# A third buffer for the gated products, some rescales moved to ScalarE, and a convolution of 28 block products in two parts

## The chip, the cores and the metric

The kernel runs on one core of a Trainium2 chip. A core has a matrix engine (TensorE, PE in the profile; its weight loads are shown apart as PEld), a vector engine (VectorE, DVE), a scalar engine (ScalarE, ACT), a general engine (GpSimd, POOL) and a queue engine (SyncE, SP). PE reads its operands from on-chip memory (SBUF) and writes into accumulators (PSUM) of 8 banks, each 128 partitions by 512 float32. The metric is the time of one execution in microseconds on the device; before the change it is 2197.08 us, the median of 3 runs (2196.97 to 2197.81).

## The reference

The input is two sequences of 1024 rows with 1024 features, so 2048 rows. One "macaron" layer is computed in float32:

```python
x = x + 0.5 * ffn(layernorm(x))
x = x + s4(layernorm(x))
x = x + 0.5 * ffn(layernorm(x))
```

`ffn` is `(silu(x @ Wg) * (x @ Wu)) @ Wd`, with Wg and Wu of 1024 x 2752 and Wd of 2752 x 1024. The weights come as 4-bit numbers, eight in a word, with a scale and a zero point for each group of 128 input rows and each column: `W = (w4 - (z4 + 1)) * s`.

`s4` is a causal convolution along the feature axis, `irfft(rfft(u, 2L) * rfft(K, 2L), 2L)[:L] + D * u` with L = 1024. The response K comes from 64 complex poles; it is the same for all rows. A causal convolution of length 1024 is a product with a lower triangular Toeplitz matrix, and in blocks of 128 x 128 that matrix has eight different blocks, one for each distance from the diagonal.

## The kernel before

Rows are worked in blocks b of 512. The list `JOBS` (L1232) holds eight jobs, (b, 1) for the first feed-forward of a block and (b, 3) for its second; j counts them from 0. Each job has a gate/up stage (`gate_up`, L602) and a down stage (`down`, L678).

The gate/up stage has 40 steps (`STEPS`, L38): 8 waves of columns, each over 8 groups g of input rows. A wave has three tiles f of 128 hidden columns (waves 0 to 4) or two (waves 5 to 7), and each tile has two units, gate (even number) and up (odd). The last wave has one more unit, the 64 columns that are left of gate and up together. In each step each unit gets two matmuls of 512 columns, one with the low part of the input (xTl, float16) and one with the high part (xTh, float32r), into the unit's own PSUM bank. The weights in SBUF are the small integers, so after each group the bank is multiplied by the ratio of this group's scale to the next one's: this is the rescale, `scaled` (L596), on ACT (L598) or DVE (L600). Even units go to ACT and odd ones to DVE; in job 0 the unit at position 1 goes to ACT when g is a multiple of 4 (L639).

After the last group of a wave `gated` (L651) makes the product with the sigmoid for each tile: ACT makes g = silu(gate) (L653), DVE multiplies it with the up unit into hf (L656), POOL casts hf into hh (L658) and subtracts to get the low part hl (L660). hf has two buffers (`hfpool`, L101), so the third hf of a wave is written once POOL is done with the first. `gated_half` (L663) does the same for the unit of 64 + 64 columns, with hf_half from the same pool (L670) and the two parts on DVE (L672, L673).

The down stage has 2 x 22 steps (a, f). Each adds hl and hh of tile f, times the weights of f, to four banks c = 0 to 3 (L689), and each bank is rescaled after it: even c on ACT, odd c on DVE (L697).

PE works in the order in which its instructions are written into its queue, and so do ACT, DVE, POOL and SP. That order is set when the program is built: a scheduler goes by the order of the code and by when it expects operands to be ready, so that an instruction may stand some way ahead of its place in the code. Some stretches are fixed by hand with `in_order_of_writing`. Work beside the matmuls is hung on step numbers, `at(up, s, f)` and `at(dn, d, f)`; it is written before the step's matmuls. Each step also issues the load of one weight tile on SP four steps ahead (L558, L565) and its cast three steps ahead, on POOL (L576) apart from a part of job 0.

The work that hangs on steps and that the change touches:

- `first_weights` (L516): job 0 unpacks all weights; its last part falls into job 0's down stage.
- `s4_tables` (L951): in job 1, one piece a step from step 2 on, the response K and the tables of the convolution. `s4_response` (L899) makes K by a transform with a cosine and a sine table (32 passes of PE, L907), scales it, adds D and writes it to DRAM. `s4_toeplitz` (L924) reads it back so that each partition is shifted by one, turns it with two matmuls (L942) into `toeplitz`, and makes the differences `after` and `ahead` (L949).
- In jobs 1, 2, 5 and 6 the s4 of the block before: for each tile t of 128 rows, the normalization at step 8 + 4t, the transposes `turn_whole` at step 10 + 4t and `convolve` (L961) at step 12 + 4t; in job 1 all of it 30 steps later. So `convolve` runs 16 times.

`convolve` makes the first four output blocks with four products (L968; 512, 384, 256 and 128 columns wide) and the last four with thirteen (L987): products of the diagonal kind, products with differences of blocks, and three products with sums of neighbouring input blocks, which POOL makes (L980). All are float32, which PE runs as two passes each. Counted in blocks of 128 columns they are 31 block products. DVE adds the results to x with three instructions (L976, L1003, L1006). PSUM banks that no unit holds are handed out in turn (`bank`, L111).

Of the kernel before, what the change touches and what calls it, by code (L numbers as in the profile page):

```python
# [23 lines left out]
P = 128  # L24
# [30 lines left out]
def macaron_s4_kernel(  # L55
# [45 lines left out]
    hfpool = ctx.enter_context(tc.tile_pool(name="hf", bufs=2))  # L101
# [500 lines left out]
    def gate_up(j, b, hooks):  # L602
        hi, lo = pieces[b]
        ps = {}
        for s, (wi, g) in enumerate(STEPS):
# [13 lines left out]
            for k, pos, done in turns:  # L619
# [18 lines left out]
                if g < GK - 1:  # L638
                    on_act = unit % 2 == 0 or (j == 0 and pos == 1 and g % 4 == 0)  # L639
# [38 lines left out]
    def down(j, b, hooks):  # L678

        steps = [(a, f) for a in range(NH) for f in range(NF)]  # L680
        for d, (a, f) in enumerate(steps):
# [5 lines left out]
            for c in range(4):  # L687
# [9 lines left out]
                on_act = c % 2 == 0  # L697
# [20 lines left out]
    toeplitz = const.tile([P, HID], F32, tag="toeplitz", name="toeplitz")  # L718

    blocks = toeplitz.rearrange("p (d m) -> p d m", d=NC)  # L720
    after = const.tile([P, 3, P], F32, tag="after", name="after")
    ahead = const.tile([P, 3, P], F32, tag="ahead", name="ahead")
# [176 lines left out]
    def s4_response():  # L899
# [4 lines left out]
        ps = bank("s4_k")  # L904
        for r in range(8):
            for i in range(2):
                nc.tensor.matmul(  # L907
                    ps[:, r : r + 1],
                    tables[i].rearrange("p (a r) -> p r a", r=8)[:, r, :],
                    s4["se"][:, i, r : r + 1],  # L910
                    start=(i == 0),
                    stop=(i == 1),
                )
        k = t4("s4_response")
        d, none = k[:1, 8:9], k[:1, P : 2 * P - 1]
        nc.sync.dma_start(d, dskip.unsqueeze(0))
        nc.gpsimd.memset(none, 0.0)
        nc.vector.tensor_scalar(k[:, :8], ps[:, :8], 1.0 / HID, None, ALU.mult)
        nc.vector.tensor_tensor(k[:1, 0:1], k[:1, 0:1], d, ALU.add)
        nc.sync.dma_start(k_dram[:, : P - 1], none)  # L920
        nc.sync.dma_start(k_dram[0, P - 1 :].rearrange("(a r) -> a r", r=8), k[:, :8])
        s4.clear()

    def s4_toeplitz():  # L924

        both = [t4("s4_rows"), t4("s4_turn")]
        rows, turn = both[0], both[1][:, :P]
# [12 lines left out]
        for i in range(NH):  # L940
            ps = bank(f"s4_t{i}")
            nc.tensor.matmul(ps, turn, rows[:, bass.ts(i, 512)], start=True, stop=True)  # L942
            dst = toeplitz[:, bass.ts(i, 512)]
            if i:
                nc.vector.tensor_copy(dst, ps)
            else:
                nc.scalar.copy(dst, ps)
        for dst, d in ((after, 3), (ahead, 1)):
            nc.vector.tensor_tensor(dst, blocks[:, d : d + 5 : 2], blocks[:, 2:7:2], ALU.subtract)  # L949
# [11 lines left out]
    def convolve(b, t, s, name):  # L961
# [4 lines left out]
        ps = bank(f"pc_{name}_0")  # L966
        for c in range(4):
            nc.tensor.matmul(  # L968
                ps[:, P * c :],
                s[:, c, :],  # L970
                toeplitz[:, : 512 - P * c],
                start=(c == 0),
                stop=(c == 3),
            )
        part = x[b][t][:, :512]
        nc.vector.tensor_tensor(part, part, ps, ALU.add)  # L976

        sums = ypool.tile([P, TB], F32, tag="y", name=f"sums_{name}")
        sums = sums[:, : 3 * P].rearrange("p (c t) -> p c t", c=3)
        nc.gpsimd.tensor_tensor(sums, s[:, 0:6:2, :], s[:, 1:6:2, :], ALU.add)  # L980
        own = bank(f"pc_{name}_1")
        both = bank(f"pc_{name}_2")[:, : 2 * P].rearrange("p (y m) -> p y m", y=2)
        flat = own.rearrange("p (y m) -> p y m", y=4)
        upper, lower = flat[:, 0:4:2], flat[:, 1:4:2]
# [4 lines left out]
        for y in range(2):  # L989
            product(flat[:, 2 * y : 2 * y + 2], s[:, 4 + 2 * y, :], blocks[:, 0:2], start=(y == 0))  # L990
        for y in range(2):
            product(flat[:, 2 * y + 1], s[:, 5 + 2 * y, :], blocks[:, 0])
        for i in range(3):
            y = slice(max(0, i - 1), 2)
            d = slice(max(0, 1 - i), 3 - i)
# [238 lines left out]
    def fast():  # L1234
        for j, (b, k) in enumerate(JOBS):
# [7 lines left out]
            if prev:  # L1243
# [3 lines left out]
                if pk == 1:  # L1247
# [11 lines left out]
                    def conv(t):  # L1259
                        convolve(pb, t, s4x.pop(t), f"{pb}_{t}")  # L1260
# [211 lines left out]
```

## Time and profile before

| what | value |
|---|---|
| median of 3 runs | 2197.08 us |
| the profiled execution, its span | 2195.57 us, 2193.7 us |
| rescales in gate/up on ACT, on DVE | 1224 of 660 ns, 1184 of 694 ns |
| rescales in down on ACT, on DVE | 640 of 662 ns, 640 of 698 ns |
| hf (DVE), hh and hl (POOL) | 168 of 749 ns, 623 ns and 1297 ns |
| passes of the convolution, 512 / 384 / 256 / 128 columns | 32 / 32 / 288 / 192 |
| granted PE clock over the run | 0.993 |

Busy times of PE can overlap, since the end of a matmul is modelled and the next one starts before it; the distance from start to start tells what one costs. A line of the timeline gives the start, the length, the engine, the source line, the operation, the tiles written and read, how many instructions are merged, and in brackets how long the engine stood before it and what released it. A line of the waits gives who waited for whom, the microseconds in total, how many times, and the longest.

### The profile page before, as it was taken

What the parts mean: (1) busy time and instruction counts of PE and PEld (TensorE: products, weight loads), DVE (VectorE), ACT (ScalarE), POOL (GpSimd) and SP (SyncE); (2) the same over time, 40 slices, a digit from 0 to 9 for tenths busy, and PEclk for the clock granted to TensorE, in tenths of its full rate; (3) what the DMA queues carried; (4) which work ended last, traced back from release to release, by engine and by line L of the source; (5) the groups of instructions that cost most, each with busy time, mean ns of one, the idle gap of its engine ahead of it and who ended that gap; (6) DMA issues with size and microseconds to landing.
All of it is one profiled execution on the core that took longest, in us unless ns stands there. A gap on an engine that the chain in (4) does not pass through costs nothing.

```text
span 2193.7 us, 29717 instructions
## 1 busy us (share of the span) xinstructions
PE 2119.6 (97%) x9524; PEld 1421.1 (65%) x9524; DVE 1720.4 (78%) x2826; ACT 1404.9 (64%) x2197; POOL 1015.0 (46%) x1334
## 2 busy tenths in 40 slices
PE   5999899999999999999999999999999999999998
PEld 3555665566867568655775558676686766865576
DVE  7889889778887877778777787867778677777776
ACT  5877466446754677666767667646776466767765
POOL 3868734444334453455334553435534345345642
PEclk9999999999999999999999999999999999999999
DMA  4433321112111211211321121112111121121111
GB/s 139 120 96 111 105 69 32 54 49 74 38 40 46 93 45 46 79 34 33 107 71 46 31 71 35 41 51 72 37 34 42 49 93 36 54 81 36 33 33 57
DMA packets 163681, 132.43 MB, mean 60 GB/s; under 512 B 22395, under 2 KB 151172, under 8 KB 163518
## 3 DMA queue, kind: packets, MB, share of 16 engines
q1 hardware_dynamic: 162670, 129.12, 19.4%
q8 instruction: 77, 1.26, 0.2%
q10 hardware_dynamic: 592, 1.25, 0.1%
q14 instruction: 86, 0.70, 0.1%
q0 software_dynamic: 256, 0.10, 0.0%
HBM read 104.79 MB, written 25.50 MB: 59 GB/s over the span
## 4 chain that ended last, share of the span: by engine, by line
PE 84%; DVE 7%; POOL 4%; issue 2%; DMA 1%; SPq 1%; ACT 0%; POOLq 0%; DVEq 0%; ACTq 0%
PE pg L628 50%; PE po L689 26%; PE pc L987 3%; DVE pg L600 2%; PE pc L968 1%; PE pb L711 1%; POOL hl L660 1%; PE pt L219 1%; DVE po L600 1%; DVE hf L656 1%; POOL w_up L576 1%; PE st L219 1%; POOL w_down L576 1%; POOL hh L658 1%; DVE rawd L461 0%
## 5 line engine op out<-in xcount | busy, mean ns | idle before, releaser
L598 ACT ACTIVATE pg<-pg,rat 128x512 f32<-128x512 f32 x1224 | 778.6, 660 | 472.3 <-PE pg L628 471.3
L600 DVE TENSOR_TENSOR pg<-pg,rat 128x512 f32<-128x512 f32 x1184 | 788.0, 694 | 167.5 <-PE pg L628 163.2
L628 PE MATMUL pg<-xTh,w_up 128*128 128x512 f32 x2752 | 878.5, 444 | 11.9 <-DVE pg L600 9.4
L628 PE MATMUL pg<-xTl,w_up 128*128 128x512 f16 x2752 | 731.1, 384 | 14.7 <-DVE w_up L572 6.6
L576 POOL CAST w_up<-b 128x768 fp32r<-128x768 int8 (+2 forms) x487 | 376.0, 774 | 614.0 <-PE pg L628 470.6
L628 PEld LDWEIGHTS pg<-xTh,w_up 128*128 128x128 f32 x2752 | 519.7, 190 | 203.0 <-DVE pg L600 41.7
L689 PE MATMUL po<-hl,w_down 128*128 128x512 f32 x1344 | 540.6, 405 | 15.4 <-DVE po L600 9.7
L598 ACT ACTIVATE po<-po,ratd 128x512 f32<-128x512 f32 x640 | 421.4, 662 | 175.1 <-PE po L689 175.1
L689 PE MATMUL po<-hh,w_down 128*128 128x512 f32 x1344 | 523.6, 393 | 0.0
L600 DVE TENSOR_TENSOR po<-po,ratd 128x512 f32<-128x512 f32 x640 | 441.6, 698 | 93.6 <-PE po L689 89.1
L628 PEld LDWEIGHTS <-w_up 128*128 128x128 bf16 x2752 | 228.3, 99 | 344.1 <-issue 165.2
L576 POOL CAST w_down<-bd 128x512 fp32r<-128x512 int8 x352 | 220.6, 628 | 422.3 <-PE po L689 366.2
L689 PEld LDWEIGHTS po<-hl,w_down 128*128 128x128 f32 x1344 | 252.9, 189 | 94.1 <-DVE po L600 23.9
L689 PEld LDWEIGHTS po<-hh,w_down 128*128 128x128 f32 x1344 | 254.0, 189 | 46.0
L660 POOL TENSOR_TENSOR hl<-hf,hh 128x512 fp32r<-128x512 f32 x168 | 218.0, 1297 | 7.9
L656 DVE SCALAR_TENSOR_TENSOR hf<-pg,rat,g 128x512 f32<-128x512 f32 x168 | 124.2, 749 | 86.7 <-ACT g L653 44.6
L653 ACT ACTIVATE g<-pg,rat 128x512 f32<-128x512 f32 x168 | 111.0, 687 | 45.9 <-PE pg L628 36.3
L658 POOL CAST hh<-hf 128x512 fp32r<-128x512 f32 x168 | 104.7, 623 | 61.4 <-PE pg L628 41.1
L182 DVE BATCH_NORM_STATS2 stats<-x 128x6 f32<-128x512 f32 x96 | 63.6, 677 | 1.0
L219 PE MATMUL pt<-ident,xn 128*128 128x128 f32 x256 | 44.2, 293 | 10.3 <-ACT xn L1339 7.6
L242 DVE TENSOR_TENSOR xTl<-pt,xTh 128x512 f16<-128x512 f32 x56 | 38.3, 688 | 13.7 <-ACT xTh L241 12.9
L219 PEld LDWEIGHTS pt<-ident,xn 128*128 128x128 f32 x256 | 34.8, 151 | 21.1 <-ACT xn L1339 9.2
(163 smaller groups left out, 957.2 us busy)
## 6 DMA issues: line engine op xcount, KB each, us to landing
b<-wq SPq DMA_DIRECT2D x319, 96.0 KB
bd<-wdq SPq DMA_DIRECT2D x336, 64.0 KB
x<-in_L_attn_u_dram SPq DMA_DIRECT2D x30, 512.0 KB
b<-wq SPq DMA_DIRECT2D x128, 64.0 KB
xs<-x SPq DMA_DIRECT2D x16, 512.0 KB
x<-xs SPq DMA_DIRECT2D x16, 512.0 KB
out_dram<-x SPq DMA_DIRECT2D x16, 512.0 KB
b<-wq SPq DMA_DIRECT2D x64, 80.0 KB
```

What stands on the lines that cost most here:

```text
L182: nc.vector.bn_stats(stats[:, t, i, :], x[b][t][:, bass.ts(i, 512)])
L219: nc.tensor.transpose(ps[:, bass.ts(k, P)], n[:, bass.ts(k, P)], ident)
L576: nc.gpsimd.tensor_copy(t, b)
L598: nc.scalar.activation(dst, src, AF.Copy, scale=sc)
L600: nc.vector.tensor_tensor(dst, src, sc.to_broadcast([P, TB]), ALU.mult)
L628: nc.tensor.matmul(p, weights, (lo, hi)[k][:, g, :], start=(g == 0 and not done), stop=(g == GK - 1 and done), skip_group_check=True,)
L653: nc.scalar.activation(g, pg, AF.Silu, scale=rat[:, 2 * f, GK - 1 :])
L656: nc.vector.scalar_tensor_tensor(hf, pu, last, g, ALU.mult, ALU.mult)
L658: nc.gpsimd.tensor_copy(hi, hf)
L660: nc.gpsimd.tensor_tensor(lo, hf, hi.bitcast(F32), ALU.subtract)
L689: nc.tensor.matmul(ps[c], w[:, bass.ts(c, P)], part, start=(f == 0 and k == 0), stop=(f == NF - 1), skip_group_check=True,)
L987: nc.tensor.matmul(dst, lhsT, rhs, start=start, stop=stop, skip_group_check=True)
```

## The change

Five edits:

- `hfpool` gets three buffers instead of two.
- In gate/up, job 1 sends the rescale of position 1 to ACT in steps 0 to 31 when g is even (16 rescales). Job 0 stays as it was.
- In the down stage of job 0, the rescale of c = 1 goes to ACT when f is even (20 rescales; the step f = 20 has none).
- The convolution is built from 28 block products in 24 matmuls: 4 of 256 columns, 20 of 128. It is a generator in two parts. The first (output blocks 0 to 3, 7 products) runs at the old step, the second (output blocks 4 to 7, 17 products) one step later. POOL makes three instructions of sums instead of one, and DVE adds the results with two instructions in the first part and three in the second. The tables are `near`, `after`, `ahead` and `middle` instead of the whole `toeplitz`, made once from the same rows.
- The response is made as one row on one partition, with its operands swapped on PE, in two banks of 512 with one evacuation each, and goes to DRAM as one row.

In the general path, which runs only when the inputs are out of range, one small tile moves to another pool and the convolution's parts run one after the other.

```diff
-    hfpool = ctx.enter_context(tc.tile_pool(name="hf", bufs=2))
+    hfpool = ctx.enter_context(tc.tile_pool(name="hf", bufs=3))
...
-                    on_act = unit % 2 == 0 or (j == 0 and pos == 1 and g % 4 == 0)
+                    on_act = unit % 2 == 0
+                    if pos == 1:
+                        on_act = (j == 0 and g % 4 == 0) or (j == 1 and s < 32 and g % 2 == 0)
...
-                on_act = c % 2 == 0
+                on_act = c % 2 == 0 or (j == 0 and c == 1 and f % 2 == 0)
...
-        ps = bank("s4_k")
-        for r in range(8):
-            for i in range(2):
-                nc.tensor.matmul(
-                    ps[:, r : r + 1],
-                    tables[i].rearrange("p (a r) -> p r a", r=8)[:, r, :],
-                    s4["se"][:, i, r : r + 1],
...
+        for half in range(2):
+            ps = bank(f"s4_k{half}")
+            for r in range(4):
+                for i in range(2):
+                    nc.tensor.matmul(
+                        ps[:1, bass.ts(r, P)],
+                        s4["se"][:, i, 4 * half + r : 4 * half + r + 1],
+                        tables[i].rearrange("p (a r) -> p r a", r=8)[:, 4 * half + r, :],
...
+            nc.vector.tensor_scalar(
+                k[:1].rearrange("p (a r) -> p r a", r=8)[:, 4 * half : 4 * half + 4],
...
-        nc.sync.dma_start(k_dram[0, P - 1 :].rearrange("(a r) -> a r", r=8), k[:, :8])
+        nc.sync.dma_start(k_dram[:, P - 1 :], k[:1])
...
+        blocks = whole.rearrange("p (d m) -> p d m", d=NC)
+        nc.vector.tensor_copy(near[:, 0:3], blocks[:, 0:3])
+        nc.vector.tensor_copy(near[:, 3], blocks[:, 4])
         for dst, d in ((after, 3), (ahead, 1)):
-            nc.vector.tensor_tensor(dst, blocks[:, d : d + 5 : 2], blocks[:, 2:7:2], ALU.subtract)
+            own = dst[:, 0:3]
+            nc.vector.tensor_tensor(own, blocks[:, d : d + 5 : 2], blocks[:, 2:7:2], ALU.subtract)
+            nc.vector.tensor_tensor(dst[:, 3], dst[:, 2], dst[:, 1], ALU.subtract)
+            nc.vector.tensor_tensor(dst[:, 2], dst[:, 0], dst[:, 1], ALU.subtract)
+        for i in range(2):
+            src = blocks[:, 2 + 4 * i]
+            nc.vector.tensor_tensor(middle[:, i], src, blocks[:, 4], ALU.subtract)
...
-        nc.gpsimd.tensor_tensor(sums, s[:, 0:6:2, :], s[:, 1:6:2, :], ALU.add)
+        nc.gpsimd.tensor_tensor(sums[:, 0:3], s[:, 0:6:2, :], s[:, 1:6:2, :], ALU.add)
+        nc.gpsimd.tensor_tensor(quad, s[:, 0:2, :], s[:, 2:4, :], ALU.add)
+        nc.gpsimd.tensor_tensor(sums[:, 3], sums[:, 0], sums[:, 1], ALU.add)
...
+        for o in range(2):
+            if o:
+                yield
+            own = bank(f"pc_{name}_{o}")
+            flat = own.rearrange("p (d m) -> p d m", d=4)
+            mine = s[:, 4 * o : 4 * o + 4]
+            product(flat[:, 0:2], mine[:, 0], near[:, 0:2], start=True)
+            product(flat[:, 1], mine[:, 1], near[:, 0])
+            product(flat[:, 2:4], mine[:, 2], near[:, 0:2])
+            product(flat[:, 3], mine[:, 3], near[:, 0])
+            product(flat[:, 3], mine[:, 0], after[:, 0])
+            product(flat[:, 2], mine[:, 1], ahead[:, 0], stop=(o == 0))
+            both = bank(f"pb_{name}_{o}")
+            if o == 0:
+                product(both[:, :P], sums[:, 0], near[:, 2], start=True, stop=True)
+            else:
+                for y in range(2):
+                    product(flat[:, 2 * y + 1], s[:, 2 - 2 * y], after[:, 2 + y])
+                    product(flat[:, 2 * y], s[:, 3 - 2 * y], ahead[:, 2 + y], stop=(y == 1))
+                twice = both.rearrange("p (y m) -> p y m", y=4)
+                product(twice[:, 0], sums[:, 1], middle[:, 0], start=True)
+                product(twice[:, 1], sums[:, 0], middle[:, 1])
+                product(twice[:, 1], sums[:, 2], near[:, 2])
+                for y in range(2):
+                    product(twice[:, y], sums[:, 3], near[:, 3])
+                product(twice[:, 3], quad[:, 0], after[:, 1])
+                product(twice[:, 2], quad[:, 1], ahead[:, 1], stop=True)
+            part = x[b][t][:, bass.ts(o, 512)]
+            nc.vector.tensor_tensor(part, part, own, ALU.add)
+            part = part.rearrange("p (y h m) -> p y h m", y=2, h=2)
+            if o == 0:
+                part = part[:, 1]
+                add = both[:, :P].unsqueeze(1).to_broadcast([P, 2, P])
+                nc.vector.tensor_tensor(part, part, add, ALU.add)
+            else:
+                add = twice[:, 0:2].unsqueeze(2).to_broadcast([P, 2, 2, P])
+                nc.vector.tensor_tensor(part, part, add, ALU.add)
+                add = twice[:, 2:4].unsqueeze(1).to_broadcast([P, 2, 2, P])
+                nc.vector.tensor_tensor(part, part, add, ALU.add)
...
                     def conv(t):
-                        convolve(pb, t, s4x.pop(t), f"{pb}_{t}")
+                        parts[t] = convolve(pb, t, s4x.pop(t), f"{pb}_{t}")
+                        next(parts[t])
...
                         at(up, late + 12 + 4 * t, lambda t=t: conv(t))
+                        at(up, late + 13 + 4 * t, lambda t=t: next(parts[t], None))
```

## The prediction

> **What bounds the kernel now.** I read the busy shares first, then the busy time of each engine by stage, then who waited for whom, and last the timeline at three places. The page says that TensorE (PE) is the bound, and VectorE (DVE) the next engine:
>
> ```profile
> span 2193.7 us, 29717 instructions
> PE 2119.6 (97%) x9524; PEld 1421.1 (65%) x9524; DVE 1720.4 (78%) x2826; ACT 1404.9 (64%) x2197; POOL 1015.0 (46%) x1334
> ```
>
> So time goes in two ways only: fewer PE cycles, or fewer places where PE waits. The view of busy time by stretch, cut at the first matmul of each stage, tells where PE waits. The columns are the stretch, its length, then busy time of PE, PEld, DVE, ACT, POOL, the granted clock and the DMA share. The second and third lines are the down stage of job 0 and the gate/up stage of job 1; the fourth is the down stage of job 3, the last two gate/up of job 5 (with four convolutions) and of job 7 (with none):
>
> ```profile
> core 0: us, PE busy (x) PEld busy (x) DVE busy (x) ACT busy (x) POOL busy (x), PEclk, DMA share, GB/s
> 204.90:313.00 108.10, 97.06 (x395) 69.62 (x394) 91.94 (x176) 59.58 (x93) 63.97 (x89) 0.95 0.28 87
> 313.00:526.70 213.70, 206.66 (x924) 128.09 (x924) 171.65 (x306) 114.74 (x179) 89.82 (x110) 0.98 0.16 48
> 1054.10:1140.10 86.00, 84.92 (x394) 68.67 (x392) 67.19 (x100) 59.50 (x93) 31.54 (x48) 1.00 0.20 58
> 1388.30:1577.90 189.60, 188.81 (x872) 120.99 (x872) 144.87 (x246) 112.77 (x178) 86.62 (x107) 1.00 0.16 51
> 1939.60:2098.50 158.90, 158.39 (x704) 94.79 (x704) 117.46 (x176) 110.44 (x174) 81.93 (x103) 1.00 0.16 48
> ```
>
> Job 0's down stage has the matmuls of job 3's and takes 22.1 us longer; job 1's gate/up takes 24.1 us more than job 5's. There DVE is over 80% busy (the one-time unpacking and the response chain), and ACT is not. From job 2 on PE is nearly gapless, and what is left shows in the waits (us in total, times, longest):
>
> ```profile
> DVE hf L656 <- POOL hl L660: 37.5, 37, 2.1
> DVE hf_half L670 <- POOL hl L660: 6.6, 8, 0.8
> PE pg L628 <- DVE pg L600: 14.6, 29, 2.1
> PE po L689 <- DVE po L600: 9.7, 20, 1.1
> PEld po L689 <- DVE po L600: 23.9, 41, 1.5
> ```
>
> DVE stands 44.1 us in 45 places because hf has two buffers and POOL must finish hl of the first before a third may be written. The timeline at the start of job 5's down stage shows how this reaches PE:
>
> ```profile
> 1579.54 1.28 POOL L660 TENSOR_TENSOR hl<-hf,hh 128x512 fp32r<-128x512 f32 x1
> 1580.86 0.76 DVE L670 SCALAR_TENSOR_TENSOR hf_half<-pg,rat,g_half 64x512 f32<-64x512 f32 x1 [0.83 <-POOL hl L660]
> 1581.65 0.70 DVE L600 TENSOR_TENSOR po<-po,ratd 128x512 f32<-128x512 f32 x1
> 1582.40 0.50 PE L689 MATMUL po<-hl,w_down 128*128 128x512 f32 x1 [0.68 <-DVE po L600]
> ```
>
> hl ends, hf_half starts, the rescale stands behind it, and PE waits for the rescale.
>
> **The change part by part.** Durations are of the profiled execution (2195.57 us, of which 2193.7 is the span). It lies 1.5 under the median of the three runs, so the sum is made against it and 1.5 added.
>
> (a) Third hf buffer. No instruction is added. It removes waits at five wave ends a job (waves 0 to 4, three tiles each) and at the end of wave 7 (two tiles and the half tile). At the down start it frees DVE 0.83 us earlier; PE stands there 1.9 us a job (two steps of 2.7 and 3.2 us for 1.8 and 2.3 of products; the chain has 32 of them in 7.31 us, 0.228 each), so 8 x 0.83 = 6.6 us go. What is late next there is DVE's own work on the half tile (0.76, 0.63 and 0.81 us), so about 1 us a job stays. After wave 4 the steps have four units, not six, and PE lost 0.8 us in every job (step of 2.60 us against 1.79): 8 x 0.8 = 6.4 us, where the third hf can now start when g is ready, 1.7 us earlier. Behind the other wave ends a step of six units takes 2.7 us of PE against 2.1 us of rescales, and mostly absorbs the wait; in the jobs with convolutions I see 0.4 to 0.7 us lost after waves 0 and 3, some 3 us together, and in jobs 0 and 1 several more that DVE's other work would cause anyway. Ends: 8 us (the scheduler's order puts other DVE work there) and 22 us (also jobs 0 and 1). I take 16.
>
> (b) Convolution, 16 times. From the timeline of one convolution a pair of passes of 256 columns takes 0.43 us and of 128 columns 0.22 us:
>
> ```profile
> 652.42 0.60 PE L987 MATMUL pc<-after,st 128*128 128x256 f32 x2
> 652.85 0.59 PE L987 MATMUL pc<-ahead,st 128*128 128x256 f32 x2
> 654.15 0.39 PE L987 MATMUL pc<-after,st 128*128 128x128 f32 x2
> 654.37 0.39 PE L987 MATMUL pc<-ahead,st 128*128 128x128 f32 x2
> 654.59 1.25 PE L987 MATMUL pc<-toeplitz,sums 128*128 128x256 f32 x6
> 655.68 0.81 PE L628 MATMUL pg<-xTl,w_up 128*128 128x512 f16 x3
> ```
>
> Old: from 648.95 to 655.68, 6.73 us for 31 blocks of 128 columns in 17 products. New: part one has 2 products of 256 and 5 of 128, 2 x 0.43 + 5 x 0.22 = 1.96 us; part two has 2 and 15, 4.16 us; 6.12 together. PE gains 0.61 x 16 = 9.8 us.
>
> A rule speaks against this. The Trainium skill, page "TensorE: Matmul & The Clock Gate", section "Part 3: Packing small matmuls — row/col tiling", says that weight loads run beside matmuls only when their row groups differ (its Part 2 also names a background buffer), and its section "LDWEIGHTS (loading the stationary operand)" prices a load of 128 columns at 128/1.2 = 107 ns. Seven more products would by that pay 14 more loads, an estimate of 1.5 us each time and 24 us in all, and the sum would be 14 us worse instead of 9.8 better. The trace does not agree for these tiles: passes of 128 columns follow each other by 0.11 us with a load of 190 ns recorded beside each.
>
> What part (b) adds beside PE: DVE gets five adds for three, one of 256 columns (0.41 us, between 0.55 for 128x384 and half of 0.69) and one more of 0.69, so 1.1 us a time; POOL two sums more, about 0.7 and 0.4 us by columns from 1.00 for 128x384. POOL's sums ran 2.5 to 3.3 us before the convolution in 12 of 16 cases, so 1.1 us more is hidden; in job 1 two of four ended 2.9 and 3.0 us after its start. The old first use came 5.6 us after it, the new one 8 blocks or 1.74 us after it: up to 1.3 us lost, twice. The second part moves one step later; with it go 17 products and three adds, past one weight load on SP and one cast on POOL that neither need nor hold them, and no DMA of its own. The wait it adds is at its end: the first rescale of the next products stood behind one add (655.88, then statistics, 657.22), now behind two. It ended at 657.90 and its bank was wanted at 658.59, so 0.69 us more just fits with six units a step. In job 1 the steps have four units (1.8 us), and 0.9 us is lost, four times. I take 5 us for all this, so (b) nets 5; ends -6 (0.7 us lost each time and the two late sums) and 9.8.
>
> (c) Response and tables, once, in job 1. The 32 passes that use the strided cosine table as weights are 0.238 us apart, 7.6 us. Turned round, the strided table moves and one column is loaded: between 0.110 (plain passes of 128 columns) and 0.238 a pass. Nearest is the same table at the same stride, so I take no gain; the other end is 4.1 us. Two evacuations of about 0.7 for one of 0.17, and some 2 us of small copies and differences, load DVE; if PE sees them, -3. The DMA of the response goes as one row of 4 KB instead of 128 of 32 bytes, on SP and not on PE's path. I take 0.
>
> (d) Job 0's down stage: 20 rescales go from DVE (0.698) to ACT (0.662): 14.0 us off DVE's 91.9 of 108.1, 13.2 on ACT's 59.6. On an even f ACT then has three in a row, 1.99 us against 1.82 of products, and 1.32 on the next. PE waited here for DVE in 5.4 us (rescales and xn), and PEld in 8.6 more that partly overlap; the rest of the 22 is POOL, DMA and a clock of 0.95. Ends 0 and 10; I take 5.
>
> (e) Job 1, steps 0 to 31: 16 rescales to ACT, 11 us off a DVE that is busy for 91.9 of the 107.0 us up to 420. Of the 24 us that this stage loses, 4 are the strided passes and part is (a). Ends 0 and 9; I take 4.
>
> The code of the general path, where one tile moves to another pool, does not run here. Sum: 16 + 5 + 0 + 5 + 4 = 30. 2195.6 - 30 = 2165.6, as a median 2167.
>
> **Rivals.** First, the buffer frees DVE but PE does not notice, because DVE's own work of the half tile and ACT's g (DVE waited 44.6 us for g) is late next. For it speaks that 29 PE waits on pg hold only 14.6 us; against it, that the idle of DVE stands right before the late rescale. (a) is then 4: 2179.
>
> Second, all good ends come true: 22 + 9.8 + 4.1 + 10 + 9 = 55, 2142; with some of it about 2150. For it speaks the clock of 0.95 in the two late stages, which rises when PE stops waiting.
>
> Third, the slower one: part one of the convolution waits for POOL. The products on sums come 3.9 us earlier than before, and at steps 16 and 24 POOL has three hh/hl pairs (1.9 us each). If the sums are queued behind them, PE stands there with its queue in order, and every rescale of the step behind it. Against the gains of 35 without (b)'s loss, it decides from 2.2 us a convolution; at 3 us it costs 48: 2210. Against it: in 14 of 16 cases the sums were done before the convolution began.
>
> Fourth, no change: (a) as in the first rival and (b) at its bad end, with nothing from (d) and (e): 4 - 6 + 0, 2199 or the same within noise.
>
> **How the numbers follow.** The forecast (2157 to 2178) has 0.45, the first rival 0.20, the second 0.17, the third 0.12, the fourth 0.06. The ends of all parts give -1 to 55, so 2142 to 2198; the range 2148 to 2197 leaves out the third rival and a part of the second. About 0.2% (4.4 us) is what a measurement of this kernel can tell from no change. Faster by more: the forecast and the first two, 0.82; within it 0.05; slower 0.13.
>
> **What would show it.** Right: the wait of hf and hf_half on POOL hl gone or under 5 us; PE idle at the down start under 0.3 us in one piece; a convolution's products summing to 6.1 us; job 0's down stage near 103 us and job 1's gate/up under 205; job 7's gate/up and down, where only the buffer acts, shorter by 1.5 us or so. Wrong: PE waiting on POOL sums, passes of 128 columns further apart than 0.11 us when 15 products follow each other, PE waits on rescales right after part two, or ACT ending PE's waits in job 0's down stage.

## The result, and the profile after

| | median us | runs |
|---|---|---|
| before | 2197.02 | 2195.92 to 2197.81 |
| after | 2164.74 | 2163.3 to 2166.51 |

The ratio is 0.9858, with a 95% interval of 0.9845 to 0.9870: about 31 us less (32.3 between the medians). The forecast was 2167 and its range 2148 to 2197. The profiled execution took 2165.84 us, of which 2164.1 is the span. The busy shares of the kernel after:

```profile
span 2164.1 us, 30241 instructions
...
PE 2097.0 (97%) x9748; PEld 1429.4 (66%) x9748; DVE 1723.0 (80%) x2831; ACT 1422.9 (66%) x2233; POOL 1038.7 (48%) x1366
```

PE has 224 more matmuls, narrower ones, and is busy 22.6 us less; DVE is as busy as before. The same stages follow by stretch, but one boundary needs care. In the kernel after, four matmuls of job 1's gate/up stand in PE's queue ahead of the last of job 0's down stage, the first of them at 304.06 us with 24 down matmuls behind it:

```profile
304.06 0.39 PE L628 MATMUL pg<-xTl,w_up 128*128 128x512 f16 x1
304.10 0.58 PE L691 MATMUL po<-hl,w_down 128*128 128x512 f32 x1
...
310.49 0.39 PE L691 MATMUL po<-hb,w_down 128*128 128x512 f32 x1
```

So the first two stretches are cut at 310.7, behind the last down matmul (before, no such matmul stands ahead, and the first of gate/up is the right place). The columns are length, then PE, PEld, DVE, ACT, POOL, clock, DMA, in the order of the lines shown of before: job 0 down, job 1 gate/up, job 3 down, job 5 gate/up, job 7 gate/up.

```profile
core 0: us, PE busy (x) PEld busy (x) DVE busy (x) ACT busy (x) POOL busy (x), PEclk, DMA share, GB/s
202.40:310.70 108.30, 96.00 (x399) 71.52 (x398) 87.20 (x162) 73.22 (x117) 65.28 (x89) 0.94 0.30 88
310.70:519.40 208.70, 199.49 (x976) 128.32 (x975) 163.82 (x301) 120.28 (x193) 93.94 (x118) 0.99 0.15 44
1037.80:1123.20 85.40, 85.01 (x394) 68.54 (x392) 67.35 (x100) 59.34 (x93) 31.88 (x48) 1.00 0.20 58
1368.90:1555.20 186.30, 186.15 (x928) 123.31 (x928) 149.39 (x254) 112.77 (x178) 91.97 (x115) 1.00 0.17 52
1912.40:2069.60 157.20, 157.20 (x706) 95.11 (x705) 117.68 (x176) 110.40 (x174) 81.87 (x103) 1.00 0.16 48
```

In gate/up of jobs 5 and 7 PE has no gap left (186.15 of 186.30, 157.20 of 157.20). Job 0's down stage is **no shorter** than before (108.3 us for 108.1, with 0.9 us in it for the four early matmuls, by 0.23 each), though one of the five edits aims at it. Job 1's gate/up takes 208.7 us for 213.7, so about 4 less with the four early matmuls added to it. (Cut at 304.1, the two would read 101.7 and 215.3; the expectations below go by these.) The waits after (total, times, longest):

```profile
PE po L691 <- DVE po L600: 11.4, 12, 3.5
...
PE pg L628 <- DVE pg L600: 8.6, 9, 3.8
...
PE po L691 <- DVE s_vc L760: 3.1, 1, 3.1
PE pb L993 <- POOL sums L988: 1.7, 1, 1.7
...
PEld po L691 <- DVE po L600: 24.3, 42, 4.0
...
DVE hf L658 <- ACT g L655: 39.9, 61, 1.0
```

No wait of hf or hf_half on POOL hl (44.1 us before) is left; the writer of hf now waits for ACT's g alone. PE's waits on the rescales of gate/up went from 14.6 us in 29 places to 8.6 in 9.

A long wait costs PE more than its own length. From 202 to 520 us PE stands over 3 us in one piece four times, and with each goes a stretch of 3.4 or 6.8 us in which the granted clock is 0.50. The one behind the wait of 3.1 us, which ends at 288.64:

```profile
289.20:292.60 3.40, 3.40 (x9) 2.50 (x8) 2.35 (x18) 1.94 (x4) 0.62 (x1) 0.50 0.42 143
```

There the matmuls start up to 0.43 us apart instead of 0.23, so by an estimate another 1.7 us (half of 3.4) are lost. Job 1's gate/up before the change holds 10.2 us at this clock (344.9 to 348.3 and 413.2 to 420.0).

### The profile page after: what moved, and what is told of

Read it like the earlier page. It is cut to its first block, busy times and chain, and to the rows that moved or that the text cites. A ratio compares the mean times of both kernels' runs of the same rounds, so it can differ in the third digit from the quotient of the medians.

```text
span 2164.1 us, 30241 instructions
## 1 busy us (share of the span) xinstructions
PE 2097.0 (97%) x9748; PEld 1429.4 (66%) x9748; DVE 1723.0 (80%) x2831; ACT 1422.9 (66%) x2233; POOL 1038.7 (48%) x1366
## 3 DMA queue, kind: packets, MB, share of 16 engines
q8 instruction: 79, 1.29, 0.3%
q10 hardware_dynamic: 592, 1.25, 0.2%
## 4 chain that ended last, share of the span: by engine, by line
PE 86%; DVE 8%; DMA 2%; POOL 2%; issue 1%; ACT 0%; SPq 0%; DVEq 0%; POOLq 0%; ACTq 0%
PE pg L628 52%; PE po L691 27%; PE pc L993 3%; DVE pg L600 2%; PE pb L713 1%; PE pb L993 1%; DVE po L600 1%; PE pt L219 1%; PE st L219 1%; DVE hf L658 1%; POOL qd L510 1%; DMA raw<-in_L_ffn_up_qweight_dram 0%; PE s_k L915 0%; ACT g L655 0%; DVE hb L674 0%
## 5 line engine op out<-in xcount | busy, mean ns | idle before, releaser
L598 ACT ACTIVATE pg<-pg,rat 128x512 f32<-128x512 f32 x1240 | 786.5, 660 | 435.7 <-PE pg L628 435.0
L600 DVE TENSOR_TENSOR pg<-pg,rat 128x512 f32<-128x512 f32 x1168 | 776.2, 693 | 168.3 <-PE pg L628 163.5
L628 PE MATMUL pg<-xTh,w_up 128*128 128x512 f32 x2752 | 855.1, 438 | 8.3 <-DVE pg L600 6.0
L628 PE MATMUL pg<-xTl,w_up 128*128 128x512 f16 x2752 | 722.8, 383 | 12.4 <-DVE w_up L572 6.6
L691 PE MATMUL po<-hl,w_down 128*128 128x512 f32 x1344 | 542.7, 406 | 15.5 <-DVE po L600 11.4
L598 ACT ACTIVATE po<-po,ratd 128x512 f32<-128x512 f32 x660 | 431.9, 662 | 167.7 <-PE po L691 167.3
L600 DVE TENSOR_TENSOR po<-po,ratd 128x512 f32<-128x512 f32 x620 | 427.1, 697 | 94.1 <-PE po L691 89.9
L660 POOL CAST hh<-hf 128x512 fp32r<-128x512 f32 x168 | 106.2, 632 | 63.3 <-PE pg L628 37.1
L1023 DVE TENSOR_TENSOR x<-x,pc 128x512 f32<-128x512 f32 x32 | 22.0, 686 | 36.4 <-PE pc L993 36.4
```

What stands on the lines that cost most here:

```text
L598: nc.scalar.activation(dst, src, AF.Copy, scale=sc)
L600: nc.vector.tensor_tensor(dst, src, sc.to_broadcast([P, TB]), ALU.mult)
L628: nc.tensor.matmul(p, weights, (lo, hi)[k][:, g, :], start=(g == 0 and not done), stop=(g == GK - 1 and done), skip_group_check=True,)
L660: nc.gpsimd.tensor_copy(hi, hf)
L691: nc.tensor.matmul(ps[c], w[:, bass.ts(c, P)], part, start=(f == 0 and k == 0), stop=(f == NF - 1), skip_group_check=True,)
```

## The experiments

### Each part alone, put into the kernel before

The buffer. Three hf buffers do not fit by themselves: pool y wants 8 KB of each partition and 7.9 KB are left. The move of the small tile z of the general path, which looks like tidying in the diff, makes the room. So the part alone is both lines:

```diff
-    hfpool = ctx.enter_context(tc.tile_pool(name="hf", bufs=2))
+    hfpool = ctx.enter_context(tc.tile_pool(name="hf", bufs=3))
...
-            z = small.tile([P, P], I32, tag="z", name=f"z_{name}")[96:P, : n // 8]
+            z = t2(f"z_{name}").bitcast(I32)[96:P, : n // 8]
```

> The kernel before with three hf buffers; the small tile of the general path moves to the other pool, as in the change, because three buffers do not fit without it. Theory A (the forecast's term a): 16 us faster than the kernel before, 2180, with no wait of hf or hf_half on POOL hl. Theory A' (what is left of the whole gain when the convolution's 8.3, the down stage's 7.3 and 0.6 measured alone are taken off, if parts add up): 15 us, 2181. Rival B (PE does not notice): 4 us or less. Rival D (the convolution and the buffer need each other): under 12 us, and the parts alone sum to less than the whole.

Measured: 2174.01 us, ratio 0.9903 (0.9888 to 0.9918), 22.2 us less. The buffer alone is two thirds of the gain, at the top end of its term.

The convolution with the response, and no other edit that runs:

```diff
-    (convolve, s4_toeplitz, s4_response and their hooks of before)
+    (those of after)
```

> The kernel before with the new convolution and response alone (two hf buffers, old split of the rescales). Theory A: 9.8 us of PE less and 5 us lost to late sums and to the two adds behind part two, so 5 us faster, 2192. Rival B (the adds and sums cost nothing): 10 us faster, 2187. Rival C (part one waits for POOL behind hh and hl, as in the slower rival of the prediction): not faster, 2197 or more, with PE waits on POOL sums of over 2 us a time.

Measured: 2187.87 us, ratio 0.9965 (0.9951 to 0.9979), 8.3 us less.

The rescales of job 0's down stage:

```diff
-                on_act = c % 2 == 0
+                on_act = c % 2 == 0 or (j == 0 and c == 1 and f % 2 == 0)
```

> The kernel before with the 20 rescales of job 0's down stage on ACT and nothing else. Theory A: 5 us faster, 2192, that stage 103 us for 108.1. Rival B (POOL, DMA and PE's own order limit this stage): within 1 us of before, with the stage at 108 and DVE's idle time in it longer.

Measured: 2188.88 us, ratio 0.9970 (0.9957 to 0.9982), 7.3 us less. In the profile, job 0's down stage takes 105.4 us to its last matmul, for 108.1, and job 1's gate/up 209.9 for 213.8: more of the gain lies behind the stage than in it.

The rescales of job 1's gate/up stage:

```diff
-                    on_act = unit % 2 == 0 or (j == 0 and pos == 1 and g % 4 == 0)
+                    on_act = unit % 2 == 0
+                    if pos == 1:
+                        on_act = (j == 0 and g % 4 == 0) or (j == 1 and s < 32 and g % 2 == 0)
```

> The kernel before with 16 rescales of job 1 on ACT in steps 0 to 31 and nothing else. Theory A: 4 us faster, 2193, job 1's gate/up 210 us for 213.7. Rival B (job 1's lost time is the response chain and single DVE pieces in the static order, not DVE's mean load): within 1.5 us of before. In the changed kernel this stage took 215.3 us, which speaks for B.

The stage has 64 steps, 8 waves of 8 groups (not 40, as said at the start), so this edit touches its first half. Measured: 2195.50 us, ratio 0.9997 (0.9988 to 1.0006): nothing. The waits within job 1's gate/up stage say why. First the kernel before, from 310 to 525 us:

```profile
PE pg L628 <- DVE pg L600: 5.0, 9, 1.9
PE pb L711 <- ACT y L598: 1.0, 1, 1.0
PE pg L628 <- DVE e L202: 0.6, 1, 0.6
```

Then the kernel with this edit alone, in the same window:

```profile
PE pg L628 <- DVE pg L600: 6.0, 7, 1.9
PE pb L713 <- ACT y L598: 1.0, 1, 1.0
PE pg L628 <- DVE e L202: 0.6, 1, 0.6
```

DVE has 16 rescales less, and PE waits for its rescales as long as before (6.0 us against 5.0). All that PE waits for in this stage is some 7 us. The stage is 24 us longer than job 5's mostly because PE is busy longer in it (206.66 against 188.81, in the lines shown of before): it has the 32 passes of the response besides, and the stretches at half clock lengthen its matmuls.

### What of the convolution counts

Both parts in one step, that is, without the split:

```diff
                     def conv(t):
-                        parts[t] = convolve(pb, t, s4x.pop(t), f"{pb}_{t}")
-                        next(parts[t])
+                        for _ in convolve(pb, t, s4x.pop(t), f"{pb}_{t}"):
+                            pass
...
-                        at(up, late + 13 + 4 * t, lambda t=t: next(parts[t], None))
```

> The changed kernel with both parts of the convolution in one step. The work is the same. If the split gives nothing: 2165 as the changed kernel. If part two's adds right behind part one keep DVE back, or one long stretch of products lets the rescales wait: slower by 0.2 to 0.5 us each of 16 times, 2168 to 2173. If the long stretch is a cover for DVE's work at wave ends: faster by up to 0.3 us each time, 2160.

Measured: 2164.35 us, ratio 0.9855 (0.9840 to 0.9870), the same as after. The split neither costs nor brings anything that shows; what is left to count is three block products fewer. One convolution of job 5 in the timeline of the kernel after:

```profile
1404.66 1.47 PE L993 MATMUL pc<-near,st 128*128 128x256 f32 x8
...
1406.42 0.39 PE L993 MATMUL pb<-near,sums 128*128 128x128 f32 x2
1406.64 0.81 PE L628 MATMUL pg<-xTl,w_up 128*128 128x512 f16 x3
...
1409.33 1.47 PE L993 MATMUL pc<-near,st 128*128 128x256 f32 x8
...
1413.32 0.39 PE L993 MATMUL pb<-ahead,quad 128*128 128x128 f32 x2
1413.55 0.81 PE L628 MATMUL pg<-xTl,w_up 128*128 128x512 f16 x3
```

Part one takes 1406.64 - 1404.66 = 1.98 us, part two 1413.55 - 1409.33 = 4.22, together 6.20 against 6.73 before. The next products start 0.23 us after the last pass, with no wait.

The response. In after, the cosine and sine tables are read at a stride of eight elements as the moving operand. Here POOL first copies them to unit stride:

```diff
+        plain = [t4("s4_pc").rearrange("p (r a) -> p r a", r=8), t4("s4_ps").rearrange("p (r a) -> p r a", r=8)]
+        for i in range(2):
+            nc.gpsimd.tensor_copy(plain[i], tables[i].rearrange("p (a r) -> p r a", r=8))
...
-                        tables[i].rearrange("p (a r) -> p r a", r=8)[:, 4 * half + r, :],
+                        plain[i][:, 4 * half + r, :],
```

> The changed kernel with the cosine and sine tables first copied by POOL into rows of unit stride, so that the 32 passes of the response move 128 neighbouring columns. If the stride of 32 bytes is what spaces these passes by 0.232 us: 0.110 each, 3.9 us less in job 1, 2161. If a pass with one row of weights is slow in itself: 0.232 as before and no gain, or a loss of a microsecond where PE waits for POOL.

Measured: 2162.24 us, ratio 0.9848 (0.9834 to 0.9861), some 2 us less than after, with intervals that overlap. The passes themselves leave no doubt. A line of a tile's instructions gives count, shortest, median and longest in ns, and the first and last start. After:

```profile
L915 PE MATMUL s_k<-s_tc,s_work x16: 389/411/412, 398.2 to 404.9; 128*1 128x128 f32 x16
...
L915 PE MATMUL s_k<-s_ts,s_work x16: 411/412/412, 398.7 to 405.4; 128*1 128x128 f32 x16
```

With plain tables:

```profile
L918 PE MATMUL s_k<-s_pc,s_work x16: 270/273/273, 396.7 to 399.9; 128*1 128x128 f32 x16
...
L918 PE MATMUL s_k<-s_ps,s_work x16: 272/273/273, 396.9 to 400.1; 128*1 128x128 f32 x16
```

32 passes start within 7.2 us in the first (0.232 us apart), within 3.4 us in the second (0.11 us apart). It is the stride of the table that costs, whether the table is loaded as weights (0.238 before) or moves.

### What is late next at the start of a down stage

The prediction said that about 1 us a job stays, behind DVE's own work on the half tile. The timeline after, at the start of job 5's down stage:

```profile
1556.75 0.76 DVE L672 SCALAR_TENSOR_TENSOR hf_half<-pg,rat,g_half 64x512 f32<-64x512 f32 x1
1557.54 0.70 DVE L600 TENSOR_TENSOR po<-po,ratd 128x512 f32<-128x512 f32 x1
1558.27 0.69 DVE L674 CAST hb<-hf_half 64x512 fp32r<-64x512 f32 x1
1558.99 0.70 DVE L600 TENSOR_TENSOR po<-po,ratd 128x512 f32<-128x512 f32 x1
1559.72 0.91 DVE L675 TENSOR_TENSOR hb<-hf_half,hb 64x512 fp32r<-64x512 f32 x1
...
1559.75 0.50 PE L691 MATMUL po<-hl,w_down 128*128 128x512 f32 x1 [0.39 <-DVE po L600]
```

hf_half starts without a wait, but it, a cast and a difference alternate with the rescales, and the second rescale, which PE waits for, ends at 1559.69. So the cast and the difference go to POOL:

```diff
-        nc.vector.tensor_copy(both[high], hf[high])
-        nc.vector.tensor_tensor(both[low], hf[high], both[high].bitcast(F32), ALU.subtract)
+        nc.gpsimd.tensor_copy(both[high], hf[high])
+        nc.gpsimd.tensor_tensor(both[low], hf[high], both[high].bitcast(F32), ALU.subtract)
```

> The changed kernel with the cast and the difference of the half tile on POOL instead of DVE. The forecast said that with the third buffer DVE's own work on the half tile is what is late next at the down start, and 1.2 us a job is still lost there (steps of 3.08 and 2.25 us for 2.26 and 1.82 of products). If that is so: 0.6 to 1.2 us a job, 5 to 9 us in all, 2156 to 2160. Rival (the order of the first rescales, or POOL, is late): within 1.5 us of the changed kernel, or slower, since POOL has three hh and hl to make there.

Measured: 2155.43 us, ratio 0.9815 (0.9801 to 0.9828), 9 us less than after, with an interval clear of it. The two instructions, by the view of that tile:

```profile
L674 POOL CAST hb<-hf_half x8: 608/609/614, 207.3 to 2065.4; 64x512 fp32r<-64x512 f32 x8
...
L675 POOL TENSOR_TENSOR hb<-hf_half,hb x8: 1277/1286/1293, 208.7 to 2066.8; 64x512 fp32r<-64x512 f32 x8
```

The difference takes longer on POOL (1.29 us against 0.91), and PE doesn't wait for it. The waits of PE on rescales of down banks fell from 11.4 us in 12 places to this:

```profile
PE po L691 <- DVE po L600: 7.2, 6, 2.6
```

The down stages of jobs 2 to 6 went from 85.4 to 84.3 or 84.4 us. Both this and the plain tables:

> The changed kernel with both the half tile on POOL (9.3 us faster alone) and the tables of unit stride (2.5 us faster alone). They act in different places, the down starts and one step of job 1. If they add up: 2153. If the one-time order of job 1 shifts again: between 2151 and 2156.

Measured: 2152.92 us, ratio 0.9806 (0.9793 to 0.9819): the two add up.

### Why the parts do not add up

Alone they sum to 22.2 + 8.3 + 7.3 + 0.6 = 38.4 us; together they give 31 or 32, so 6 or 7 us are missing. The intervals of the five runs together leave this figure uncertain by some 6 us, so in the medians it is barely clear of the noise. I took the length of each stage in all profiles, with the boundary behind the last matmul of the down stage; the difference lies in jobs 0 and 1. By the profiles 3.8 us are missing in job 0's gate/up, where kernels that do the same differ by up to 2 us, and 5.9 in the two stages after it; the later stages give some back. Two kernels ask which edit it is: after without the rescales of job 1, and after without those of job 0's down stage.

```diff
-                    on_act = unit % 2 == 0
-                    if pos == 1:
-                        on_act = (j == 0 and g % 4 == 0) or (j == 1 and s < 32 and g % 2 == 0)
+                    on_act = unit % 2 == 0 or (j == 0 and pos == 1 and g % 4 == 0)
```

> The changed kernel without the 16 rescales of job 1 on ACT. Alone that edit gave 0.6 us, within the noise. If it is worth nothing beside the others too: 2164 to 2166. If it helps once the buffer has taken the waits away: slower, 2168. If it is part of why job 1's gate/up became 1.5 us longer in the changed kernel than before, because ACT's load or the changed order does harm there: faster, 2160 to 2162.

```diff
-                on_act = c % 2 == 0 or (j == 0 and c == 1 and f % 2 == 0)
+                on_act = c % 2 == 0
```

> The changed kernel without the 20 rescales of job 0's down stage on ACT. Alone that edit gave 7.3 us, buffer and convolution alone 22.2 and 8.3, the three together 7 less than their sum. If the down edit keeps its worth: 2172. If the overlap lies in it (the buffer alone already took 3.0 us from that stage and 4.6 from the one before): 2164 to 2168.

Measured: without job 1's rescales 2161.08 us, ratio 0.9845 (0.9832 to 0.9859); without job 0's 2166.36 us, ratio 0.9868 (0.9853 to 0.9883). Both intervals overlap that of after. The stages of one profile each, in us:

| kernel | job 0 down | job 1 gate/up | both |
|---|---|---|---|
| before | 108.1 | 213.8 | 321.9 |
| buffer alone | 105.1 | 212.8 | 317.9 |
| convolution alone | 108.1 | 212.0 | 320.1 |
| job 0's rescales alone | 105.4 | 209.9 | 315.3 |
| job 1's rescales alone | 109.5 | 213.9 | 323.4 |
| after without job 1's | 105.7 | 205.9 | 311.6 |
| after without job 0's | 106.2 | 210.9 | 317.1 |
| after | 108.3 | 208.7 | 317.0 |

(In after, with and without job 1's rescales, four gate/up matmuls or 0.9 us count to the down stage; with job 0's rescales alone it is one.)

Against before, the buffer gives 4.0 us in these two stages, the convolution 1.8, job 0's rescales 6.6, and job 1's lose 1.5. Without job 1's rescales the other three give 10.3 of their 12.4. Without job 0's, the others give 4.8 where their sum is 4.3. All together give 4.9 where the sum is 10.9. By these single profiles most of the loss comes only with both sets of rescales in. The medians say so less clearly: by them 3.8 us are missing without job 1's, 2.4 without job 0's and 6 with both, each uncertain by some 6 us. With both sets in, job 0's rescales gain nothing in their own stage (108.3 us with them, 106.2 without), nor in the two together.

The waits of job 1 give a candidate. In after PE stands 3.77 us in one piece at 383 us, behind a rescale that stands on DVE behind seven small operations of the tables; without job 1's rescales the longest there is 0.7 us, and without job 0's it is there too (3.74 us). The order of DVE's instructions differs. So the pieces of the tables were held in the order in which they are written:

```diff
-                    at(up, s, lambda: next(tables, None))
+                    piece = lambda: in_order_of_writing(lambda: next(tables, None), ET.DVE)
+                    at(up, s, piece)
```

> The changed kernel with the pieces of the response chain held to their place in DVE's order (each piece behind the DVE instruction written just before it). In the changed kernel eleven small pieces stand before the first rescales after wave 2 of job 1, each as long as POOL's hl beside it, and PE waits 3.77 us for the rescale. If that order is the cause of job 1's loss: PE's wait there is gone and job 1's gate/up takes 211 to 213 us for 215.3, 2161 to 2163. If the pieces cost the same wherever they stand: 2164 to 2166, or slower where one now holds a rescale that it stood behind before.

Measured: 2158.33 us, ratio 0.9833 (0.9819 to 0.9846), 5 us less than after with intervals that just touch, but not for the reason given. The wait that it aimed at is still there, in the waits from 370 to 390 us of this kernel:

```profile
PE pg L628 <- DVE pg L600: 3.7, 1, 3.7
```

Job 0's down stage now takes 101.7 us for 108.3, job 1's gate/up 210.3, both 312.0 for 317.0. What went is a wait of 3.1 us in job 0's down stage (from 195 to 310 us, PE waits for the down banks only as below, and no more for DVE's s_vc) and the wait of 1.7 us for POOL's sums:

```profile
PE po L691 <- DVE po L600: 7.9, 4, 3.5
...
PE po L691 <- ACT po L598: 1.0, 3, 0.4
```

In after, DVE stood 3.64 us for a DMA of the one-time work there:

```profile
287.36 0.29 DVE L807 TENSOR_TENSOR s_vc<-s_vc 128x128 f32<-128x128 f32 x1 [3.64 <-DMA s_vc<-in_L_attn_Bp_dram]
...
287.90 0.69 DVE L600 TENSOR_TENSOR po<-po,ratd 128x512 f32<-128x512 f32 x1
288.50 0.15 DVE L760 TENSOR_SCALAR s_vc<-s_vc 128x1 f32<-128x1 f32 x1
```

Two small instructions after it comes a rescale, and PE goes on at 288.64, right after that rescale. (The waits put PE's 3.1 us down to the s_vc instruction that ends in the same moment; by the time, it is the rescale, and behind it the DMA.)

With the pieces held in their order, the same instruction starts in job 1's gate/up and waits for nothing:

```profile
L807 DVE TENSOR_TENSOR s_vc<-s_vc x1: 291/291/291, 362.9 to 362.9; 128x128 f32<-128x128 f32 x1
```

So in after the scheduler had put this instruction of job 1's tables into job 0's down stage, where its data had not landed yet, and the rescales queued behind it waited, and PE with them. The wait and the stretch at half clock behind it, 3.1 + 1.7 us, are about what this run gained. The other profiles show that DVE's wait for this load moves with the other edits: 1.4 us before, 1.2 with job 0's rescales alone, 2.3 in after without job 1's, 3.6 in after; without job 0's it is gone, and DVE waits 1.6 us for another load of the same work. That this is what the two sets of rescales do to each other is argued and not shown; why the order falls as it does stays open.

Last, all that helped, in one kernel: the half tile on POOL, plain tables, no rescales of job 1, tables in the written order.

> The changed kernel with the half tile on POOL, the tables of unit stride, the pieces of the response chain held to their place in DVE's order, and without the 16 rescales of job 1 on ACT. Measured one by one against the kernel before, these were worth 9.3, 2.5, 5.4 and 2.7 us beyond the changed kernel. If they add up: 2144 to 2146. The order and the rescales both act on the waits in jobs 0 and 1 (3.1 us on the first pole instruction, 3.8 us after wave 2), so part of them is likely the same: 2146 to 2150. If the order of job 1 falls differently again: 2153 as without them.

Measured: 2151.21 us, ratio 0.9801 (0.9787 to 0.9814), the fastest of all, some 12 us below after. It is about 1 us below the kernel with the half tile and the plain tables alone, although the last two edits gave 3 and 5 us by themselves: they remove the same loss, or less than their single runs said. Neither wait at issue is as it was: the first pole instruction waits for nothing here, and the longest wait of PE on a rescale of gate/up is 2.1 us. But PE's waits on these rescales are then 12.8 us in 17 places, against 8.6 in 9 in after.

## Why the prediction was right, point by point

| term | forecast (ends) | alone, with interval | taken from after |
|---|---|---|---|
| (a) buffer | 16 (8 to 22) | 22.2 (18.0 to 24.6) | |
| (b) + (c) convolution, response | 5 + 0 | 8.3 (4.6 to 10.8) | |
| (d) job 0 down | 5 (0 to 10) | 7.3 (4.0 to 9.4) | 2 |
| (e) job 1 | 4 (0 to 9) | 0.6 (-1.3 to 2.6) | -3 |
| sum | 30 | 38.4 | |

The time was right to 2.3 us, the sum of 30 to 1 or 2, and partly by luck, since errors cancel: taken alone, (a), (b) and (d) came out above their terms (only for (a) clear of its interval), (e) below, and the sum left out that parts overlap (6 or 7 us).

**(a)** The mechanism held: the waits on hl went, and PE's waits with them. Job 7's gate/up, where only the buffer acts, became 1.7 us shorter (158.9 to 157.2) and its down stage 0.7 (95.2 to 94.5); 1.5 was promised for both. The step that was too small is that behind the other wave ends a step of six units "mostly absorbs the wait": with the buffer alone, gate/up of jobs 3, 4 and 7 gained 2.3, 1.8 and 1.7 us where 0.8 had been counted after wave 4. At the down start the promise was slightly too large: the two steps take 3.08 and 2.25 us for 2.26 and 1.82 of products, so 1.25 is lost where it was 1.9, a gain of 0.65 and not 0.83. The sign "idle under 0.3 us in one piece" failed by a little (0.39). That the half tile's own work is late next was right, and worth more than it looked: the run with it on POOL gained 9 us, eight times 1.2. Jobs 0 and 1, named for the upper end only, gave 8.6 us of the 22 in the three stages from job 0's gate/up to job 1's gate/up; job 0's gate/up differs by up to 2 us between profiles of kernels that do the same in it, so this figure is rough.

**(b)** The products took 6.20 us where 6.12 was worked out, so 0.53 x 16 = 8.5 us less for PE. The 5 us taken off for late sums and two adds were not there: PE waited for POOL's sums once, 1.73 us (until 448.82 in job 1, where "up to 1.3, twice" was priced), and not at all behind part two in job 5. The buffer gives part of that room: with the convolution alone, job 5's gate/up gained 1.4 us of the 2.1 that its four convolutions had become shorter by; with both edits it gained 3.3 us, where the buffer alone gives 1.4. The rule on weight loads of the Trainium skill, page "TensorE: Matmul & The Clock Gate", section "Part 3: Packing small matmuls — row/col tiling", would by the prediction's estimate have made this part a loss of 14 us; it gained 8. The trace was the one to follow.

**(c)** The nearest row held: 0.232 us a pass for 0.238. The reason for taking it, the stride, was shown by the copy of the tables.

**(d)** Alone the edit is worth 7.3 us where 5 was taken, but its sign failed: job 0's down stage near 103 us became 108.3 (105.4 with the edit alone). PE stands there 3.54, 3.37 and 3.09 us, twice for a rescale of DVE and once for the one behind the DMA, with half clock each time. ACT ends 0.5 us of PE's waits there, in two places. Within the whole change the edit gives 2 us, within the noise.

**(e)** This step failed: "job 1's gate/up under 205" became 208.7 with four of its matmuls done ahead, and the edit alone gave nothing. The ends "0 and 9" came from DVE's busy share and the stage's excess over job 5. The waits within that stage, asked of before, hold 5.0 us on rescales, and with 16 rescales moved they hold 6.0.

**The rivals.** The first (PE doesn't notice the buffer) falls with the run of the buffer alone. The second is not reached, though (a) alone came to its price for it. The clock that it counted on, 0.95 and 0.98 in the two late stages, did not rise: 0.94 and 0.99. In the third, PE would have stood 3 us a convolution for POOL's sums: it was 1.7 us, once in sixteen. The fourth falls with the first.

## What to carry to other kernels

An engine that is 80% busy need not give anything back when it is relieved: here 16 rescales fewer on DVE gave nothing in a stage where PE waited 5.0 us for rescales. Read PE's waits within the stage for a first idea of what there is to gain, and add the half clock that follows the long ones. Price parts that touch the same queue in the same stage together, since here they did not add up, and neither did what the last repairs gave alone. When a buffer has freed an engine, see what it does next in the same place: the two small instructions of the half tile were worth 9 us, about as much as the new convolution. And before you compare two stages by their length, see that they hold the same work: one early matmul at a boundary moved 6.6 us from one stage to the next.

## What the runs showed of the hardware

**A stride costs PE the same on either operand.** Passes of 128 columns over a float32 table at a stride of eight elements are 0.232 us apart with the table moving and 0.238 with it loaded. At unit stride it is 0.11 both times: with the plain tables moving, and in these 16 passes of the kernel after, where a float32 table of 128x128 is loaded and 8 columns move:

```profile
374.46 1.85 PE L837 MATMUL s_sums<-s_vc,s_sq 128*128 128x8 f32 x16
```

**Small DVE operations can wait for a whole POOL operation.** In after, from 380 to 386 us, DVE's operations on two inputs of 128x8 in SBUF took up to 1.23 us instead of 0.15 to 0.17, where one began while POOL was at work. The view of this tile's instructions, then the timeline:

```profile
L867 DVE TENSOR_TENSOR s_work<-s_work x28: 151/166/1234, 376.6 to 390.1; 128x8 f32<-128x8 f32 x28
```

```profile
382.13 0.20 DVE L878 RECIPROCAL s_work<-s_work 128x8 f32<-128x8 f32 x1
382.25 3.91 DVE L867 TENSOR_TENSOR s_work<-s_work 128x8 f32<-128x8 f32 x7
386.09 1.28 DVE L600 TENSOR_TENSOR pg<-pg,rat 128x512 f32<-128x512 f32 x2
...
382.15 1.28 POOL L662 TENSOR_TENSOR hl<-hf,hh 128x512 fp32r<-128x512 f32 x1
383.38 0.63 POOL L660 CAST hh<-hf 128x512 fp32r<-128x512 f32 x1
384.09 1.26 POOL L662 TENSOR_TENSOR hl<-hf,hh 128x512 fp32r<-128x512 f32 x1
385.30 0.85 POOL L576 CAST w_up<-b 128x768 fp32r<-128x768 int8 x1
...
386.83 1.09 PE L628 MATMUL pg<-xTh,w_up 128*128 128x512 f32 x3 [3.77 <-DVE pg L600]
```

Seven such operations took 3.91 us instead of about 1.1. Four of them were long, 1.21, 0.57, 1.23 and 0.79 us, and each ended within 0.03 us of the POOL instruction that it began beside. PE's wait of 3.77 us ends behind the rescale that follows them. The Trainium skill, page "SBUF — State Buffer", section "Who interferes with whom", has the mechanism: GpSimd and VectorE share a pair of ports by an exclusive lock, and the one that comes second stands until the other's whole instruction is done. The page says so of a VectorE instruction with two inputs in SBUF beside a GpSimd instruction that reads SBUF, which is the case here. The trace agrees: beside POOL's subtractions of 1.26 to 1.28 us the operations take 1.21 to 1.23, beside its cast of 0.63 us 0.57. The rescales, one of whose inputs lies in PSUM, show no such thing: 0.70 us beside POOL's work. What it costs in all was not measured by itself, since the run that was to remove this wait did not.
